# A layer norm on GpSimd that takes the mean from the statistics' tile, without a negated copy from ScalarE

## The chip, the cores and the metric

The kernel runs on one core of one Trainium2 chip. The metric is the device time of one execution in microseconds (us); the time before is 1062.31 us, the median of three runs (1062.3 to 1063.7).

The core has five engines that work side by side, each through its own queue in order: PE (TensorE, matrix products; its weight loads are listed apart as PEld), DVE (VectorE), ACT (ScalarE), POOL (GpSimd) and SP (SyncE, which here only issues DMAs). An instruction that waits for another engine holds up all that stands behind it in its own queue.

## The reference, cut to what matters

Thirty-two batches of a 512 x 128 array `x` go through four graph layers. Each layer first normalizes the rows, then applies its own attention to the result, and adds what comes out to `x`:

```
def _layernorm(x, axis=-1, eps=1e-5):
    m = jnp.mean(x, axis=axis, keepdims=True)
    v = jnp.var(x, axis=axis, keepdims=True)
    return (x - m) / jnp.sqrt(v + eps)
...
h = jnp.maximum(_layernorm(x, axis=-1), 0.0)
x = x + _L0_gnn_ref(h, adj, ...)
h = jnp.maximum(_layernorm(x, axis=-1), 0.0)
x = x + _L1_gnn_ref(h, adj, ...)
... (the same with _L2_gnn_ref and _L3_gnn_ref)
```

The four layers are attention over a 512 x 512 adjacency matrix with different masks and score functions. The norm ahead of them is the same each time, so there are 4 x 32 = 128 of these norms.

## The kernel before, in words

**Tiles.** A batch is held as 128 partitions by 4 chunks (`C`) of 128 values; a partition holds four rows, and a statistic of the batch is a 128 x 4 tile. All batches stay in `xs` from load to output.

**The norm, `preln` (L530).** It has up to five steps:

- `variances` (L503): DVE computes `bn_stats` of each chunk (L511, four instructions) and `bn_aggr` (L513, four instructions). The result `mv` is 128 x 4 x 2: mean and variance side by side.
- `inv_dev` (L518): POOL adds epsilon to the variance (L523, `ve`) and raises it to the power -1/2 (L525, `rstd`).
- `emit_shift`: in the ACT variant (the first eight batches of layer 0) DVE makes -mean x rstd (L541). In the POOL variant (the other 120 norms) ACT makes -mean (L556), a tile of its own named `shift`.
- `norm`: in the ACT variant four activations (L545); in the POOL variant four `tensor_scalar` (L560), each of which adds `shift` and multiplies by `rstd`, both given as one value for each partition.
- PE turns the result `xn` over (four transposes, L421) and ACT applies the Relu on the way out of PSUM (L570, `hT`). `hT` feeds the projection on PE (L595 or L581).

**The order of the work.** The kernel does not issue its work in the order of the code. `Plan.op` collects 5421 operations, each with its engine, an assumed length, what it reads and writes, and a due time (`turn`); one norm in one layer of one batch begins a chain. `Plan.run` (L158) then walks through assumed time: of all engines it takes the operation that can begin first, within 0.05 us the one that is due first, and issues it. Every engine's queue has exactly this order. An operation that waits only for earlier work of low priority is therefore put behind whatever the plan found to be due earlier on that engine. Layer 1 of batch b begins after layer 0 of batch b + 6, layer 2 six batches later, and layer 3 four more (`LAGS`, L70).

**Buffers.** Large tiles come from rooms with a fixed count that the plan keeps account of; `xn` comes from `by_pool` (5 buffers, L320). Small tiles (`mv`, `rstd`, `shift` and others) come from `small` (L308), with 8 buffers for each name. The plan keeps no account of those: when none of the eight is free, the writing instruction waits on the chip. `mv` is taken 192 times (128 norms, and two more statistics in each batch of layer 1), `rstd` 192 times, `shift` 128 times.

Beside the chains there are preparations of the adjacency matrix and of the weights. Where the plan sees PE idle for over 0.6 us it issues transposes of the identity whose result is not used (`idle_products`, L334; 150 of them).

Of the kernel before, what the change touches and what calls it, by code (L numbers as in the profile page):

```python
# [34 lines left out]
ALU = mybir.AluOpType  # L35
# [14 lines left out]
PE, DVE, ACT, POOL, SP = "PE", "DVE", "ACT", "POOL", "SP"  # L50
# [61 lines left out]
class Plan:  # L112
# [17 lines left out]
    def op(self, engine, length, emit, reads=(), writes=(), load=0.0, transfers=0, port=0):  # L130
        slots = list(dict.fromkeys(v.slot for v in (*reads, *writes) if v.slot is not None))
        k = len(self.chains) - 1
        op = Operation(engine, length, emit, k, slots)
        op.load, op.transfers, op.port = load, transfers, port
        for s in slots:
            s.users += 1
        needs = {}
        for v in reads:
            needs.update(dict.fromkeys(v.writers))
        for v in writes:  # L140
            needs.update(dict.fromkeys(v.writers))
            needs.update(dict.fromkeys(v.readers))
        for v in reads:
            v.readers.append(op)
        for v in writes:
            v.writers.append(op)
        for n in needs:
            n.after.append(op)
            if n.chain == k:
                op.way = max(op.way, n.way + n.length + DELAY[n.engine])  # L150
        count, beside, begin, _ = self.chains[k]
        turn = begin + STRETCH * op.way if beside is None else beside[0] + beside[1] * count
        op.turn = (turn, len(self.ops))
        op.missing = len(needs)
        self.chains[-1][0] += 1
        self.ops.append(op)
# [101 lines left out]
def kernel(  # L258
# [28 lines left out]
    nc = tc.nc  # L287
# [13 lines left out]
    def wide(t):  # L301

        return t.rearrange("p c f -> p (c f)")
# [4 lines left out]
    def small(name, shape=(P, C)):  # L308
        return sm.tile(list(shape), F32, name=name, tag=name)
# [19 lines left out]
    op = plan.op  # L329
# [8 lines left out]
    def value(r, name):  # L338
        return Value(Slot(r, name))
# [57 lines left out]
    v_x = [Value() for _ in range(B)]  # L397
# [18 lines left out]
    def turn_op(dst, src, reads, writes):  # L416


        def emit():
            for k in range(C):  # L420
                nc.tensor.transpose(dst(k), src(k), ident)  # L421

        op(PE, 0.44, emit, reads, writes)
# [76 lines left out]
    def dve(length, emit, reads, writes, port=0):  # L500
        op(DVE, length, emit, reads, writes, port=port)

    def variances(src, reads):  # L503

        mv = Value()

        def emit():
            st = small("st", (P, C, 6))
            mv.own = small("mv", (P, C, 2))
            for c in range(C):  # L510
                nc.vector.bn_stats(st[:, c, :], src(c))  # L511
            for c in range(C):
                nc.vector.bn_aggr(mv.own[:, c, :], st[:, c, :])  # L513

        dve(1.1, emit, reads, [mv])
        return mv

    def inv_dev(mv):  # L518
        rstd = Value()

        def emit():
            ve = small("ve")
            nc.gpsimd.tensor_scalar(ve, mv.own[:, :, 1], LN_EPS, 1.0, ALU.add, ALU.mult)  # L523
            rstd.own = small("rstd")
            nc.gpsimd.tensor_tensor(rstd.own, ve, mhalf, ALU.pow)  # L525

        op(POOL, 1.3, emit, [mv], [rstd])
        return rstd

    def preln(b, engine):  # L530

        src = xs[:, b]
        mv = variances(lambda c: src[:, c, :], [v_x[b]])
        rstd = inv_dev(mv)
        shift = Value()
        xn = value(by_act if engine is ACT else by_pool, "xn")
        if engine is ACT:

            def emit_shift():
                shift.own = small("shift")  # L540
                nc.vector.scalar_tensor_tensor(shift.own, mv.own[:, :, 0], -1.0, rstd.own, ALU.mult, ALU.mult)  # L541

            def norm():
                for c in range(C):
                    nc.scalar.activation(  # L545
                        xn.t[:, c, :], src[:, c, :], AF.Identity, bias=shift.own[:, c : c + 1],
                        scale=rstd.own[:, c : c + 1],
                    )

            dve(0.08, emit_shift, [mv, rstd], [shift], port=1)  # L550
            op(ACT, 1.54, norm, [shift, rstd, v_x[b]], [xn])
        else:

            def emit_shift():
                shift.own = small("shift")
                nc.scalar.mul(shift.own, mv.own[:, :, 0], -1.0)  # L556

            def norm():
                for c in range(C):
                    nc.gpsimd.tensor_scalar(  # L560
                        xn.t[:, c, :], src[:, c, :], shift.own[:, c : c + 1], rstd.own[:, c : c + 1],
                        ALU.add, ALU.mult,
                    )

            op(ACT, 0.1, emit_shift, [mv], [shift])
            op(POOL, 1.72, norm, [shift, rstd, v_x[b]], [xn], port=4)
        pt = value(banks, "pt")
        turn_op(lambda k: pt.t[:, k, :], lambda k: xn.t[:, k, :], [xn], [pt])
        hT = value(by_act, "hT")
        op(ACT, 0.49, lambda: nc.scalar.activation(wide(hT.t), wide(pt.t), AF.Relu), [pt], [hT])  # L570
        return hT, pt
# [114 lines left out]

    def layer0(b):
        hT, _ = preln(b, ACT if b < EARLY else POOL)
        if b + AHEAD < B:
            load_x(b + AHEAD)  # L690
# [169 lines left out]

    def layer1(b):
        hT, _ = preln(b, POOL)
        h = project_scored(hT, w1_ext, [v_w1])
        src, v_h = Value(), Value(h[0].slot)
# [77 lines left out]
    def layer2(b):  # L942
        hT, _ = preln(b, POOL)
        h = project_scored(hT, w2_ext, [v_w2])
        po, ssum = attend(h, lambda: h[0].t[:, :, P], h, h, None, None)
        v1 = value(by_dve, "v1")

        rs = Value()

        def emit_rs():  # L950
            rs.own = small("rs")
            nc.vector.reciprocal(rs.own, ssum[0].own)

        dve(0.1, emit_rs, ssum, [rs])
        dve(0.6, lambda: nc.vector.tensor_mul(v1.t, po[0].t, per_chunk(rs.own)), [*po, rs], [v1])  # L955
        op(POOL, 1.25, lambda: nc.gpsimd.tensor_add(v1.t, v1.t, row_of(B_L2)), [v_rows], [v1], port=1)  # L956


        em = value(by_act, "em")
        op(ACT, 0.62, lambda: nc.scalar.activation(em.t, v1.t, AF.Exp, bias=minus1), [v1], [em])  # L960
        op(DVE, 0.6, lambda: nc.vector.scalar_tensor_tensor(em.t, em.t, 1.0, v1.t, ALU.min, ALU.max), [v1], [em], port=1)  # L961
        op(POOL, 1.25, lambda: nc.gpsimd.tensor_add(xs[:, b], xs[:, b], em.t), [em], [v_x[b]], port=1)  # L962
# [399 lines left out]
```

## Time and profile before

| | before |
|---|---|
| median of the runs, us | 1062.31 (1062.3, 1062.31, 1063.7) |
| span of the profiled execution, us | 1062.1 |
| median of the runs less that span, us | 0.2 |
| PE busy, us | 1041.7 |
| PEld busy, us | 966.0 |
| DVE busy, us | 868.5 |
| ACT busy, us | 780.5 |
| POOL busy, us | 776.2 |

The page gives the profiled execution's time as its span, from the first to the last instruction. "Busy" is the time in which an engine has an instruction at work; waits in its queue are not in it. A share of the whole span is an average over a start in which data arrive and the first batches fill the pipeline, a long middle, and an end in which it drains. The stretches are therefore read apart.

In a line of instruction groups stand the source line, the engine, the operation, what it writes and reads, the shape and the count; then busy time in total, the mean duration of one in ns, and the idle time of the engine just before such instructions with what ended it. In a timeline the first number is the start in us, the second the duration of the run of like instructions. A window's line gives the busy time of PE, PEld, DVE, ACT and POOL in that stretch with their instruction counts, then the clock granted to PE, the DMA share and GB/s.

### The profile page before, as it was taken

The page shows a single profiled execution, that of the slowest core. Times are in us where ns is not written, and L with a number is a line of the kernel's source. Part 1 is how long each engine was busy: PE and PEld are TensorE (multiplying, and loading weights), DVE is VectorE, ACT ScalarE, POOL GpSimd, SP SyncE. Part 2 cuts the span into 40 slices and gives each one's busy share as a digit, 9 for nine tenths or more (in the row PEclk, how much of TensorE's full clock was granted, in tenths as well). Part 3 has the DMA queues.
Part 4 walks back from the last instruction along what each step waited for, and adds up shares of the span by engine and source line. Part 5 has one row for each costly group of instructions (what it writes and reads, how often), then busy time and mean ns, then how long its engine had stood idle before and what let it go on. Part 6 is the DMA issues. An engine that isn't in the chain of part 4 may idle for free.

```text
span 1062.1 us, 25166 instructions
## 1 busy us (share of the span) xinstructions
PE 1041.7 (98%) x8475; PEld 966.0 (91%) x8475; DVE 868.5 (82%) x3694; ACT 780.5 (73%) x2024; POOL 776.2 (73%) x1140
## 2 busy tenths in 40 slices
PE   7899999999999999999999999999999999999998
PEld 7789789989999999999999999999899999999997
DVE  7799999989988878888888888888888877766752
ACT  6768897789877777777877777787777777767751
POOL 4489577778787777787778778777877666576772
PEclk9899999999999999999999999999999999999999
DMA  6400000000010000000000000000000000000001
GB/s 181 96 12 2 1 2 21 2 12 11 2 31 2 21 21 21 22 21 12 2 12 11 12 12 12 11 2 11 12 11 11 11 11 11 11 22 11 22 24 37
DMA packets 56912, 20.49 MB, mean 19 GB/s; under 512 B 21584, under 2 KB 56272, under 8 KB 56784
## 3 DMA queue, kind: packets, MB, share of 16 engines
q1 hardware_dynamic: 56784, 18.90, 7.2%
q8 instruction: 67, 1.10, 0.5%
q14 instruction: 61, 0.50, 0.2%
HBM read 10.43 MB, written 8.39 MB: 18 GB/s over the span
## 4 chain that ended last, share of the span: by engine, by line
PE 88%; DVE 4%; POOL 3%; DMA 1%; SPq 1%; issue 1%; ACT 1%; POOLq 0%; DVEq 0%; ACTq 0%
PE po L675 20%; PE pt L421 16%; PE po L984 10%; PE pg L911 10%; PE proj L595 7%; PE po L837 5%; PE prow L421 3%; PE p L581 3%; PE pz L581 3%; PE px L581 3%; PE po L980 3%; PE po L842 2%; PE po L834 1%; PE po L847 1%; POOL xn L560 1%
## 5 line engine op out<-in xcount | busy, mean ns | idle before, releaser
L675 PE MATMUL po<-h,pT 128*128 128x128 f32 x2048 | 242.8, 275 | 0.8 <-DVE pT L664 0.8
L675 PEld LDWEIGHTS po<-h,pT 128*128 128x128 f32 x2048 | 236.4, 192 | 5.8 <-issue 4.1
L560 POOL TENSOR_SCALAR xn<-xs,shift,rstd 128x128 f32<-128x128 f32 x480 | 213.1, 459 | 2.8 <-DVE top L633 0.9
L655 ACT ACTIVATE y<-y,nmax 128x512 f32<-128x512 f32 x256 | 181.7, 714 | 5.3 <-DVE nmax L637 4.6
L525 POOL TENSOR_TENSOR rstd<-ve,mhalf 128x4 f32<-128x4 f32 x160 | 170.9, 1068 | 13.3
L622 DVE CUSTOM_DVE_ANT_0 y<-prow,bias 128x512 f32<-128x512 f32 x256 | 162.8, 683 | 1.6 <-PE prow L421 1.6
L984 PE MATMUL po<-h,offT 128*128 128x128 f32 x1024 | 135.4, 275 | 0.0
L911 PE MATMUL pg<-adjTe,hg 128*128 128x512 f32 x256 | 131.0, 593 | 0.0
L421 PE MATMUL pt<-ident,y 128*128 128x128 f32 x1024 | 130.2, 274 | 0.7 <-ACT hl L819 0.7
L421 PEld LDWEIGHTS pt<-ident,y 128*128 128x128 f32 x1024 | 115.1, 141 | 13.8 <-issue 8.5
L984 PEld LDWEIGHTS po<-h,offT 128*128 128x128 f32 x1024 | 124.6, 192 | 0.0
L511 DVE BATCH_NORM_STATS2 st<-xs 128x6 f32<-128x128 f32 x512 | 109.8, 277 | 7.2 <-POOL xs L962 4.5
L595 PEld LDWEIGHTS proj<-w_ext,hT 128*128 128x128 f32 x768 | 96.8, 192 | 19.0 <-issue 9.6
L595 PE MATMUL proj<-w_ext,hT 128*128 128x130 f32 x768 | 102.9, 277 | 1.4 <-ACT hT L570 1.3
L647 ACT ACTIVATE y<-y,src 128x512 f32<-128x512 f32 x128 | 84.6, 714 | 20.8 <-DVE rmax L622 19.6
L962 POOL TENSOR_TENSOR xs<-xs,em 128x512 f32<-128x512 f32 x32 | 42.0, 1312 | 76.8 <-DVE em L961 63.8
L956 POOL TENSOR_TENSOR v<-v,rows 128x512 f32<-128x512 f32 x32 | 40.9, 1279 | 72.4 <-DVE v L955 72.4
L570 ACT ACTIVATE hT<-pt 128x512 f32<-128x512 f32 x128 | 73.5, 589 | 25.3 <-PE pt L421 14.0
L647 ACT ACTIVATE y<-y,h 128x512 f32<-128x512 f32 x128 | 84.7, 714 | 7.9 <-DVE rmax L622 7.7
L664 DVE TENSOR_TENSOR pT<-pt,adjT 128x512 f32<-128x512 f32 x128 | 82.6, 681 | 5.7 <-PE pt L421 5.6
L421 PE MATMUL pt<-ident,xn 128*128 128x128 f32 x512 | 77.8, 274 | 1.5 <-POOL xn L560 1.3
L412 ACT COPY h<-proj 128x260 f32<-128x260 f32 x192 | 66.1, 371 | 13.4 <-PE proj L595 12.4
(204 smaller groups left out, 2302.3 us busy)
## 6 DMA issues: line engine op xcount, KB each, us to landing
xs<-in_x_dram SPq DMA_DIRECT2D x32, 256.0 KB, 4.0
out_dram<-yo SPq DMA_DIRECT2D x32, 256.0 KB, 2.3
u<-h SPq DMA_DIRECT2D x128, 0.5 KB, 1.8
bias<-in_adj_dram SPq DMA_DIRECT2D x4, 256.0 KB, 4.4
wts<-in_L_gnn_W_dram SPq DMA_DIRECT2D x3, 64.0 KB, 4.2
rows<-in_L_gnn_bias_dram SPq DMA_DIRECT2D x2, 64.0 KB, 3.7
wt_o<-L_gnn_others_weight_dram SPq DMA_DIRECT2D x1, 64.0 KB, 2.5
wts<-n_L_gnn_self_weight_dram SPq DMA_DIRECT2D x1, 64.0 KB, 4.5
```

The costliest lines, as they stand in the source:

```text
L421: nc.tensor.transpose(dst(k), src(k), ident)
L511: nc.vector.bn_stats(st[:, c, :], src(c))
L525: nc.gpsimd.tensor_tensor(rstd.own, ve, mhalf, ALU.pow)
L560: nc.gpsimd.tensor_scalar(xn.t[:, c, :], src[:, c, :], shift.own[:, c : c + 1], rstd.own[:, c : c + 1], ALU.add, ALU.mult,)
L581: nc.tensor.matmul(pt.t[:, c, :], lhsT=column(hT, c), rhs=w, start=True, stop=True)
L595: nc.tensor.matmul(p[:, c, :], lhsT=column(hT, 2 * k + c), rhs=w_ext, start=True, stop=True)
L622: nc.vector.tensor_tensor_reduce(wide(y[ib].t), wide(prow.t), bias[:, ib, :], 1.0, LOWEST, ALU.add, ALU.max, rmax.own[:, ib : ib + 1],)
L647: nc.scalar.activation(yw, yw, AF.Prelu, alpha=0.2, bias=src()[:, ib : ib + 1])
L655: nc.scalar.activation(yw, yw, AF.Exp, bias=nmax.own[:, ib : ib + 1], accum_out=ssum[0].own[:, ib : ib + 1])
L675: nc.tensor.matmul(po[ib].t[:, ib, :], lhsT=pT.t[:, jb, :], rhs=h[0].t[:, jb, 0:P], start=(jb == 0), stop=(jb == C - 1),)
L911: nc.tensor.matmul(wide(pg.t), lhsT=hg.t[:, nb, :], rhs=adjTe[:, nb, :], start=(nb == 0), stop=(nb == C - 1))
L984: nc.tensor.matmul(po[ib].t[:, ib, :], lhsT=offT[:, jb, blk(ib)], rhs=h1.t[:, jb, :], start=False, stop=(jb == C - 1),)
```

## The change

In the POOL variant of `preln` the norm subtracts the mean, read from `mv`, in place of adding `shift`. The ACT operation that made `shift` is left out, and with it the norm's dependence on ACT. The norm now reads `mv` itself, so a buffer of `mv` is in use until the norm is done. The assumed length of the norm stays 1.72. The plan is made anew from the changed list of operations; the ACT variant is as it was.

```diff
@@ preln, the branch for POOL
-            def emit_shift():
-                shift.own = small("shift")
-                nc.scalar.mul(shift.own, mv.own[:, :, 0], -1.0)
-
             def norm():
                 for c in range(C):
                     nc.gpsimd.tensor_scalar(
-                        xn.t[:, c, :], src[:, c, :], shift.own[:, c : c + 1], rstd.own[:, c : c + 1],
-                        ALU.add, ALU.mult,
+                        xn.t[:, c, :], src[:, c, :], mv.own[:, c, 0:1], rstd.own[:, c : c + 1],
+                        ALU.subtract, ALU.mult,
                     )
 
-            op(ACT, 0.1, emit_shift, [mv], [shift])
-            op(POOL, 1.72, norm, [shift, rstd, v_x[b]], [xn], port=4)
+            op(POOL, 1.72, norm, [mv, rstd, v_x[b]], [xn], port=4)
```

## The prediction, made before the changed kernel was run

> **What bounds the kernel now.** I read the windows view first, because the shares of the page average over stages. Two stretches of the middle, then four of the start:
>
> ```profile
> 350.00:400.00 50.00, 50.00 (x415) 46.62 (x414) 42.10 (x159) 38.25 (x98) 34.32 (x53) 1.00 0.05 12
> 750.00:800.00 50.00, 50.00 (x422) 47.27 (x422) 40.97 (x146) 36.72 (x89) 37.83 (x54) 1.00 0.04 11
> ```
>
> ```profile
> 35.00:50.00 15.00, 11.10 (x72) 9.28 (x73) 10.80 (x69) 11.57 (x41) 6.00 (x9) 0.90 0.35 83
> 50.00:75.00 25.00, 23.43 (x180) 21.68 (x179) 22.55 (x116) 13.21 (x46) 21.88 (x37) 0.92 0.09 13
> 75.00:105.00 30.00, 29.80 (x259) 29.21 (x258) 27.81 (x122) 26.21 (x73) 29.31 (x46) 1.00 0.06 10
> 105.00:150.00 45.00, 43.16 (x318) 37.62 (x317) 44.12 (x207) 36.87 (x102) 28.42 (x36) 1.00 0.01 2
> ```
>
> In the middle PE is busy for 50.00 of 50 us, ACT for 38 and POOL for 34 to 38. Less work on ACT buys nothing there. At the start no single engine is full: to 50 us everyone has gaps (POOL works 6.00 of 15 us), from 50 to 105 us POOL is the fullest (51.2 of 55 us), from 105 us DVE (44.1 of 45). So a gain or a loss is made before 150 us or where an engine stops PE.
>
> The chain of waits says the same; POOL carries it in this stretch (norms, powers, the add of L871):
>
> ```profile
> 58.02 1.02 POOL rstd L525
> ...
> 62.23 1.15 POOL h L871
> 63.38 1.74 POOL xn L560 x4
> ...
> 65.81 1.72 POOL xn L560 x4
> ```
>
> **The change, part by part.**
>
> *Removed: 120 ACT instructions (L556).*
>
> ```profile
> L556 ACT ACTIVATE shift<-mv 128x4 f32<-128x4 f32 x120 | 23.0, 205 | 48.3 <-DVE mv L513 25.7 <-DVE rsum L791 9.9 <-POOL xn L560 9.6
> ```
>
> 120 x 205 ns is 24.6 us of durations (23.0 us busy, since neighbours overlap), and ACT stood idle for 48.3 us just before them. All of it lies beside PE, which is full; I cost it at nothing in the middle. Were that cover gone, ACT's 23.0 us would be the most it could give.
>
> *Changed: 480 POOL instructions subtract where they added, and take the mean from `mv`.* No row shows this form. The nearest rows are a subtraction and an addition of two tiles of one size on this engine:
>
> ```profile
> L820 POOL TENSOR_TENSOR hl<-hs,hl 128x256 fp32r<-128x256 f32 x64 | 46.5, 744 | 21.4 <-ACT hl L819 20.6 <-PE proj L595 0.7
> L857 POOL TENSOR_TENSOR xs<-xs,rest 128x256 f32<-128x256 f32 x32 | 24.2, 755 | 36.3 <-DVE nmax L750 16.5 <-ACT rest L852 14.9 <-DVE rs L795 2.1
> ```
>
> Subtraction costs 744 ns, addition 755 ns. So I take no difference from the 448 ns median of L560. The ends are 372 ns (half of the 744 for half the columns; 76 ns less) and 744 ns (the whole row; 296 ns more). What counts is the stretch that POOL fills: the window view of L560 has 36 of them from 50 to 105 us, so the ends are -36 x 76 ns = -2.7 us and +36 x 296 ns = +10.7 us. In the middle POOL works some 36 of 50 us, and even +296 ns for each of about 24 norms in 50 us (7.1 us) would leave it below PE.
>
> *Moved: the first norms of the POOL variant.* This is where I expect the time to change. POOL's timeline:
>
> ```profile
> 35.09 1.23 POOL L525 TENSOR_TENSOR rstd<-ve,mhalf 128x4 f32<-128x4 f32 x1
> ...
> 36.93 1.01 POOL L525 TENSOR_TENSOR rstd<-ve,mhalf 128x4 f32<-128x4 f32 x1
> 42.62 1.44 POOL L820 TENSOR_TENSOR hl<-hs,hl 128x256 fp32r<-128x256 f32 x2 [4.68 <-ACT hl L819]
> ...
> 53.06 1.75 POOL L560 TENSOR_SCALAR xn<-xs,shift,rstd 128x128 f32<-128x128 f32 x4
> ```
>
> and ACT's:
>
> ```profile
> 51.31 0.22 ACT L556 ACTIVATE shift<-mv 128x4 f32<-128x4 f32 x1
> ...
> 56.28 0.59 ACT L556 ACTIVATE shift<-mv 128x4 f32<-128x4 f32 x5
> ```
>
> Eight powers come before 33 us, for the eight ACT norms; those at 35.09 and 36.93 us are the first for norms on POOL (layer 0 of batch 8 and layer 1 of batch 0). Both are complete by 37.94 us, and POOL then stands idle for 4.68 us. Yet ACT makes the first `shift` at 51.31 us and the next five from 56.28 us: the plan put these steps behind ACT's work that was due earlier. Without them both norms are free at 37.94 us. They take 1.75 us (53.06) and 1.72 us (65.81), which the 4.68 us gap holds. So 3.5 us of work leave the packed stretch after 50 us.
>
> What is late next is DVE: it is busy for 25.80 us of the 30 from 50 to 80 us (windows view), so at most 4.2 us can be taken back there before DVE leads. A third norm (power finished at 47.96 us, `shift` among the five at 56.28) might move too, but POOL's next gap is only 1.22 us; 3.5 us is my value, 4.2 the cap. What follows a moved norm moves with it: four transposes, a Relu and a projection on PE and ACT, and for batch 8 four DMAs on SP's queue (4 x 0.6 us), which is idle from 42.22 to 47.91 us.
>
> PE had waits of 1.33 and 0.57 us at 45.5 to 47.8 us, and its granted clock was 0.90 in this stretch. Eight products of L837 take 2.07 us at 48.83 and 1.91 us at 51.12, against 1.06 us at 42.50; with their neighbours (L834, L595) the excess is 2.9 us. If the moved work fills those waits this may go too. I leave it out of the forecast and keep it for the low end.
>
> Two rows bear on where the norms land. The four of 71.55 us took 2.87 us, while DVE ran L1185, L805 and L806, each with two inputs in SBUF. The Trainium skill, SBUF — State Buffer, section Who interferes with whom, speaks against the change here: a DVE instruction with two SBUF inputs blocks a GpSimd instruction that reads SBUF, and DVE runs L805 and L806 at 40.54 us, where the norms would go. By that rule both might take 2.87 us, 5.7 us for a gap of 4.68, and about 1 us of the gain would be lost.
>
> *Added: a longer life for `mv`.* DVE's `bn_aggr` may now wait for a norm on POOL, with all of DVE's queue behind it (scores, `pT`, which PE waits for). I cost it at nothing in the forecast, and price it below.
>
> The sum is -3.5 us against the profiled execution's 1062.1 us, 0.2 us under the median; on the median it is **1058.8 us**.
>
> **The rivals.**
>
> *No change: 1062.3 us.* The early norms only stand waiting. ACT is the engine that delayed `shift`, and ACT also makes the Relu that each of them needs next; DVE is full from 105 us on and may swallow what POOL gives. Against it: ACT is busy only 13.21 of 25 us from 50 to 75 us.
>
> *Slower, by DVE waiting for a buffer of `mv`: 1068.7 us.* Statistics run far ahead: from the end of a `shift` to the start of its norm the median is 42 us. The queue orders pair statistics and norms; so paired, the trace has at most eight `rstd` in use, and eight is all there are. With `mv` held to the norm's end a ninth would be wanted at three places: statistics at 312.5 us against a norm that ends at 313.6, at 807.2 against 809.6, at 832.3 against 835.3. That is 1.0 + 2.4 + 3.0 = 6.4 us of DVE. It decides where the wait is longer than PE's store of ready work. Against it stands a wait of the same kind now:
>
> ```profile
> ACT shift L556 <- POOL xn L560: 9.6, 3, 4.5
> ```
>
> ACT waited 9.6 us for `shift` buffers, 4.5 at the longest, and PE kept on: from 300 to 316 us, around one of them, it was busy 16.00 of 16.
>
> *The subtraction is dear on GpSimd: 1073.0 us,* by the +10.7 us above. The equal pair L820 and L857 speaks against it.
>
> That the change does not do what it says would show as any of the 120 rows of L556 left over, or as a norm that still waits for ACT; I give it no chance of its own.
>
> **How the numbers follow.** About 0.2% (2.1 us) is what a measurement of this kernel can tell from no change. The forecast case has 0.46, of which 0.42 is faster by more than that and 0.04 within. No change has 0.22, of which 0.20 within and 0.02 slower. The wait for `mv` has 0.24, the dear subtraction 0.08; both are slower. Besides, the plan is made anew, and any stretch of the start may fall differently; that is why the first case has no more. Faster 0.42, within 0.24, slower 0.34. The low end is -4.2 (DVE's cap) - 2.9 (clock) = 1055.2; POOL's -2.7 us would lie under the same cap. The high end takes in the dear subtraction's bound, 1073. The likeliest case alone reaches from 1055 to 1060.
>
> **What would show it.** Right: no L556; first POOL norms at 38 to 42 us; POOL less packed from 50 to 75 us; L560 still at 448 ns; PE at 50.00 in the middle. Wrong: POOL idle at 38 to 42 us as before (then another step holds the norms), DVE's L513 waiting for POOL's L560 with PE below 50.00 at the same time, or L560 well above 448 ns.

## The result and the profile after

| | before | after |
|---|---|---|
| median of the runs, us | 1062.3 (4 runs, 1061.67 to 1063.7) | 1189.42 (4 runs, 1187.99 to 1193.06) |
| span of the profiled execution, us | 1062.1 | 1186.3 (its time: 1187.99) |

The changed kernel is slower: 1.1201 times the time of before (95% interval 1.1182 to 1.122), 127.1 us. The forecast was 1058.8 us in a range that ended at 1073.

The page of the changed kernel, busy time by engine:

```profile
PE 1084.8 (91%) x8447; PEld 985.0 (83%) x8447; DVE 882.5 (74%) x3694; ACT 764.5 (64%) x1904; POOL 946.9 (80%) x1140
```

POOL has the same 1140 instructions as before and works 170.7 us longer on them (946.9 less 776.2). ACT has the 120 instructions fewer that the diff says. The costliest group of POOL is the norm, first before, then after:

```profile
L560 POOL TENSOR_SCALAR xn<-xs,shift,rstd 128x128 f32<-128x128 f32 x480 | 213.1, 459 | 2.8 <-DVE top L633 0.9 <-DVE res L937 0.9 <-PE pt L421 0.7
```

```profile
L556 POOL TENSOR_SCALAR xn<-xs,mv,rstd 128x128 f32<-128x128 f32 x480 | 391.2, 826 | 0.5
```

(L556 was the `shift` line before; in the changed kernel this number is the norm's, L560 of before.) One norm instruction takes 826 ns on average and 792 ns at the median; before it was 459 and 448. By busy time the row grew by 178.1 us (391.2 less the 213.1 of before), which covers all of POOL's increase. (Its busy time is less than 480 x 826 ns, as neighbours overlap.)

The windows, first the two stretches of the middle, then the one of the start that the forecast was to relieve:

```profile
350.00:400.00 50.00, 48.41 (x384) 43.36 (x383) 42.38 (x162) 38.23 (x93) 44.81 (x54) 1.00 0.05 12
750.00:800.00 50.00, 45.62 (x352) 41.22 (x351) 38.34 (x147) 31.63 (x79) 41.54 (x50) 0.97 0.03 6
```

```profile
50.00:75.00 25.00, 19.80 (x150) 18.13 (x151) 16.73 (x89) 11.47 (x38) 23.86 (x31) 0.93 0.07 13
```

PE had 50.00 of 50 us in both stretches of the middle, and now has 48.41 and 45.62. The important column is the one in brackets behind it: PE gets 384 and 352 instructions done where it did 415 and 422. POOL works 45 and 42 of 50 us: more than before, and still not all of the time. From 50 to 75 us POOL is more packed and not less: 23.86 of 25 us, where it was 21.88. So an engine that is not full holds PE up. The waits view names the way:

```profile
ACT zn L922 <- POOL rstd L525: 68.3, 23, 5.0
PEld pt L421 <- POOL xn L556: 54.9, 100, 1.9
...
PE po L979 <- ACT h L412: 35.5, 12, 3.0
...
DVE mv L513 <- POOL xn L556: 12.5, 4, 4.4
```

(The columns are the us waited, how often, and the longest.) PE waits for norms directly, at its weight loads 100 times; and 12 times it waits 3 us for `h`, which ACT makes late because ACT was waiting for a power from POOL. DVE's wait for `mv`, the rival that the prediction priced at 6.4 us, is there too, but is a small part.

The first norms of the POOL variant, from POOL's timeline:

```profile
34.30 1.23 POOL L525 TENSOR_TENSOR rstd<-ve,mhalf 128x4 f32<-128x4 f32 x1
35.64 3.13 POOL L556 TENSOR_SCALAR xn<-xs,mv,rstd 128x128 f32<-128x128 f32 x4
...
40.27 3.49 POOL L556 TENSOR_SCALAR xn<-xs,mv,rstd 128x128 f32<-128x128 f32 x4
```

They begin at 35.64 and 40.27 us, where the two norms that the prediction wanted early had begun at 53.06 and 65.81; so the move that the forecast was built on did happen. But a norm (four instructions) now lasts 3.13 or 3.49 us, where it had lasted 1.75.

### The profile page after: what moved, and what is told of

Read it like the earlier page. It is cut to its first block, busy times and chain, and to the rows that moved or that the text cites. A ratio compares the mean times of both kernels' runs of the same rounds, so it can differ in the third digit from the quotient of the medians.

```text
span 1186.3 us, 25075 instructions
## 1 busy us (share of the span) xinstructions
PE 1084.8 (91%) x8447; PEld 985.0 (83%) x8447; DVE 882.5 (74%) x3694; ACT 764.5 (64%) x1904; POOL 946.9 (80%) x1140
## 5 line engine op out<-in xcount | busy, mean ns | idle before, releaser
L556 POOL TENSOR_SCALAR xn<-xs,mv,rstd 128x128 f32<-128x128 f32 x480 | 391.2, 826 | 0.5
L979 PE MATMUL po<-h,offT 128*128 128x128 f32 x1024 | 151.3, 296 | 35.5 <-ACT h L412 35.5
L525 POOL TENSOR_TENSOR rstd<-ve,mhalf 128x4 f32<-128x4 f32 x160 | 166.4, 1040 | 13.4
L979 PEld LDWEIGHTS po<-h,offT 128*128 128x128 f32 x1024 | 139.0, 211 | 37.9 <-ACT h L412 37.8
L421 PE MATMUL pt<-ident,xn 128*128 128x128 f32 x512 | 98.6, 286 | 36.6 <-POOL xn L556 33.9
L421 PEld LDWEIGHTS pt<-ident,xn 128*128 128x128 f32 x512 | 64.0, 142 | 61.3 <-POOL xn L556 54.9
L412 ACT COPY pT<-pt 128x512 f32<-128x512 f32 x64 | 35.8, 587 | 89.5 <-PE pt L421 89.5
```

The lines of the kernel that those rows point to most:

```text
L556: nc.gpsimd.tensor_scalar(xn.t[:, c, :], src[:, c, :], mv.own[:, c, 0:1], rstd.own[:, c : c + 1], ALU.subtract, ALU.mult,)
L979: nc.tensor.matmul(po[ib].t[:, ib, :], lhsT=offT[:, jb, blk(ib)], rhs=h1.t[:, jb, :], start=False, stop=(jb == C - 1),)
```

## The experiments

The diff changes three things together: the operation (subtraction for addition), the place of the operand (`mv`, a 128 x 4 x 2 tile, with the longer life of its buffers), and the order of every queue, since the plan is made anew. Theory 1: the subtraction itself is dear on this engine, wherever its scalar lies. Theory 2: the scalar's place in `mv` makes the instruction slow. Theory 3: the norm is not dearer, and the loss comes from the other order and the longer life of `mv`. Beside them stands the question how 170.7 us on an engine that is 80% busy become 127 us of the whole. Each time is set against runs of the kernel before on the same chip, with medians of 1061.87, 1062.7 and 1062.89 us in the three groups.

**1. sub_from_copy: the operation alone.** The kernel before, with its order, its queues and its `shift` tile; ACT's copy no longer negates, and POOL subtracts it.

```diff
-                nc.scalar.mul(shift.own, mv.own[:, :, 0], -1.0)
+                nc.scalar.mul(shift.own, mv.own[:, :, 0], 1.0)
...
-                        ALU.add, ALU.mult,
+                        ALU.subtract, ALU.mult,
```

> The kernel before, with two edits that cancel: ScalarE's step copies the mean without the sign, and the norm subtracts it. Order, plan and buffers are those of before; only the operation differs. Theory 1 (GpSimd's subtraction with a per-partition value is dear): the norm at about 790 ns, as in the changed kernel's 792, and a time well above 1100 us. Theory 2 (reading the mean from the statistics' tile, where it stands beside the variance, is dear): the norm at 448 ns and 1062 us. Theory 3 (the longer life of the statistics' buffers and the other order): 448 ns and 1062 us as well.

Measured: 1177.47 us, 1.1085 times before [1.1067, 1.1102], +115.6 us. The group of the norm in this kernel:

```profile
L560 POOL TENSOR_SCALAR xn<-xs,shift,rstd 128x128 f32<-128x128 f32 x480 | 390.6, 826 | 0.2
```

826 ns again, without `mv` and in the old order. Theories 2 and 3 fall as the main cause: the operation by itself costs 115.6 us in the old order. As the queues are those of before and only a duration differs, this kernel is also where to see how the time is lost. POOL's timeline of before, then of sub_from_copy, at the same place in the order:

```profile
513.48 5.17 POOL L560 TENSOR_SCALAR xn<-xs,shift,rstd 128x128 f32<-128x128 f32 x12
518.62 1.27 POOL L919 TENSOR_TENSOR hgb<-hg,rows 128x512 f32<-128x512 f32 x1
520.26 1.36 POOL L525 TENSOR_TENSOR rstd<-ve,mhalf 128x4 f32<-128x4 f32 x1
```

```profile
521.94 9.86 POOL L560 TENSOR_SCALAR xn<-xs,shift,rstd 128x128 f32<-128x128 f32 x12
531.77 1.28 POOL L919 TENSOR_TENSOR hgb<-hg,rows 128x512 f32<-128x512 f32 x1
533.74 1.03 POOL L525 TENSOR_TENSOR rstd<-ve,mhalf 128x4 f32<-128x4 f32 x1
```

The plan puts three norms in a row. They took 5.17 us and now take 9.86, and the power behind them ends 4.7 us later for it. What stands behind that power, from ACT's timeline, first of before:

```profile
521.66 1.28 ACT L927 ACTIVATE zn<-zn,rstd 128x128 f32<-128x128 f32 x4 [0.30 <-POOL rstd L525]
...
524.68 0.56 ACT L412 COPY h<-p 128x512 f32<-128x512 f32 x1
```

```profile
534.80 1.28 ACT L927 ACTIVATE zn<-zn,rstd 128x128 f32<-128x128 f32 x4 [4.97 <-POOL rstd L525]
...
537.82 0.56 ACT L412 COPY h<-p 128x512 f32<-128x512 f32 x1
```

ACT waits 4.97 us for the power in place of 0.30. The copy `h` begins 3.02 us after `zn` in both kernels, so it is late by as much. PE's timeline goes on from there, first of before:

```profile
525.63 1.06 PE L984 MATMUL po<-h,offT 128*128 128x128 f32 x8
```

```profile
538.44 1.53 PE L984 MATMUL po<-h,offT 128*128 128x128 f32 x8 [2.95 <-ACT h L412]
539.76 0.64 PE L980 MATMUL po<-wts,own 128*128 128x128 f32 x2
540.19 1.91 PE L984 MATMUL po<-h,offT 128*128 128x128 f32 x8
...
543.52 1.06 PE L984 MATMUL po<-h,offT 128*128 128x128 f32 x8
```

PE stands for 2.95 us. Its next two sets of eight products take 1.53 and 1.91 us and the third 1.13; then it is 1.06 us again, as each time at this place before. The clock column of the windows goes with it:

```profile
538.00:541.00 3.00, 2.56 (x14) 2.56 (x15) 2.04 (x10) 3.00 (x11) 2.07 (x4) 0.68 0.05 6
541.00:545.00 4.00, 4.00 (x28) 3.76 (x27) 1.13 (x8) 2.14 (x8) 4.00 (x6) 0.81 0.06 0
545.00:550.00 5.00, 5.00 (x45) 4.76 (x44) 3.78 (x18) 0.84 (x3) 3.57 (x5) 1.00 0.16 52
```

The granted clock is 0.68 and 0.81 after the wait and then 1.00. (In finer windows it is 0.50 from 540 to 542 us and 1.00 from 543 to 545.) The wait is paid for twice.

**2. add_from_mv: the order and the place, without the operation.** The changed kernel with the addition put back; it leaves out the sign of the mean.

```diff
-                        ALU.subtract, ALU.mult,
+                        ALU.add, ALU.mult,
```

> The changed kernel with the norm adding the mean where it should subtract it; this leaves the sign of the mean out of the computation. Plan, order and buffers are those of the changed kernel. Theory 1: the norm back at 448 ns; the time then is that of the rest of the change, 1058.8 us by my forecast (first norms earlier), up to 1068.7 us if VectorE's waits for the statistics' buffers reach TensorE. Theory 2: 792 ns and about 1189 us. Theory 3: 448 ns, but a time that stays near 1189 us.

Measured: 1076.24 us, 1.013 times before [1.0105, 1.0156], +14.4 us. The norm takes 463 ns, so reading `mv` costs POOL nothing. This is the kernel that the prediction believed it was forecasting, a norm at the old price in the new order, and it is slower too. The first norms, from POOL's timeline:

```profile
36.35 1.75 POOL L556 TENSOR_SCALAR xn<-xs,mv,rstd 128x128 f32<-128x128 f32 x4
...
39.57 2.17 POOL L556 TENSOR_SCALAR xn<-xs,mv,rstd 128x128 f32<-128x128 f32 x4
```

They fill the gap as forecast, in 3.9 us. What did not follow is the gain. Two windows of before, then the same of add_from_mv:

```profile
80.00:90.00 10.00, 10.00 (x88) 9.77 (x87) 9.56 (x42) 9.71 (x27) 9.83 (x18) 1.00 0.01 2
140.00:150.00 10.00, 10.00 (x92) 10.00 (x91) 9.97 (x50) 8.39 (x26) 6.36 (x11) 1.00 0.01 3
```

```profile
80.00:90.00 10.00, 6.64 (x45) 5.73 (x46) 7.19 (x30) 10.00 (x27) 9.85 (x13) 0.96 0.01 2
140.00:150.00 10.00, 5.19 (x36) 3.89 (x34) 8.12 (x37) 9.75 (x28) 5.43 (x7) 1.00 0.01 2
```

From 80 to 90 us POOL does 13 instructions in the place of 18 in the same busy time: longer ones come first. Over 0 to 150 us PE is busy for 125.62 us where it was 135.87, and from 350 to 950 us for 598.16 of 600. Of the ten us less at the start 2.6 are idle products, whose number the plan sets (110 for 131, 14.03 us for 16.65); 7.6 us are real work. So most of the loss is at the start, in an order of which the early norms are only one part.

**3. sub_true_length: the plan is told.** The changed kernel with the assumed length of the norm at its measured four times 792 ns, 3.17 us; what is computed is the same.

```diff
-            op(POOL, 1.72, norm, [mv, rstd, v_x[b]], [xn], port=4)
+            op(POOL, 3.17, norm, [mv, rstd, v_x[b]], [xn], port=4)
```

> The changed kernel, with the norm's assumed length in the plan at its measured 3.17 us (four times 792 ns) in place of 1.72. If the loss comes from queues laid out for a norm of 1.72 us, so that TensorE stands behind norms that are late, the time falls to 1080 to 1130 us. If GpSimd simply has too much to do (947 us busy), it stays within 15 us of 1189 us.

Measured: 1104.67 us, 1.0399 times before [1.0383, 1.0416]; of the 127.1 us, 42.8 are left. Its page and the middle in one window:

```profile
PE 1065.3 (97%) x8571; PEld 978.8 (89%) x8571; DVE 886.2 (80%) x3694; ACT 771.1 (70%) x1904; POOL 948.6 (86%) x1140
```

```profile
350.00:950.00 600.00, 595.16 (x4833) 547.79 (x4832) 498.13 (x2033) 436.20 (x1053) 559.12 (x664) 1.00 0.05 13
```

POOL has the same 948.6 us of work, and from 350 to 950 us it is even busier than in the changed kernel (559.12 against 496.19 of 600 us); yet PE is at 595.16 in place of 548.50. So it is not POOL's work as such that stops PE in the middle, but its place in the queues.

**4. forms: the price by itself.** The kernel before, with 88 POOL instructions added whose results nobody uses: eight of each form on tiles of 128 partitions.

```diff
+    for _ in range(8):
+        ts(to[:, 0:128], src[:, 0:128], s, m, ALU.add, ALU.mult)
+    for _ in range(8):
+        ts(to[:, 0:128], src[:, 0:128], s, m, ALU.subtract, ALU.mult)
...
+    for _ in range(8):
+        ts(to[:, 0:32], src[:, 0:32], s, m, ALU.subtract, ALU.mult)
```

> The kernel before with 88 GpSimd instructions behind its end, eight of each form, on 128 columns (the last two forms on 32): add then multiply, subtract then multiply, the same two with the first value from a tile of pairs, multiply then add, multiply then subtract, multiply twice, add or subtract then multiply with constants. Theory 1: every form with a subtraction at about 790 ns and the others at 448; the tile of pairs makes no difference. Theory 2: the two forms that read the tile of pairs at 790 ns, subtraction from the plain tile at 448. On 32 columns theory 1 expects a subtraction some 85 ns above an addition if the price goes by the column, 340 ns if by the instruction.

The added instructions stood in POOL's queue at 755 to 822 us, not at the end as meant; the span of this single run is 1109.1 us, which says nothing of the change. The answer is in the durations (least, median, most, in ns), one source line for each form:

```profile
L1338 POOL TENSOR_SCALAR biasT<-xs,one x8: 447/448/472, 755.2 to 759.1; 128x128 f32<-128x128 f32 x8
```

```profile
L1340 POOL TENSOR_SCALAR biasT<-xs,one x8: 792/792/802, 759.6 to 766.4; 128x128 f32<-128x128 f32 x8
```

```profile
L1344 POOL TENSOR_SCALAR biasT<-xs,two,one x8: 792/794/795, 771.7 to 782.4; 128x128 f32<-128x128 f32 x8
```

```profile
L1348 POOL TENSOR_SCALAR biasT<-xs,one x8: 789/792/1425, 789.1 to 798.3; 128x128 f32<-128x128 f32 x8
```

```profile
L1354 POOL TENSOR_SCALAR biasT<-xs x8: 642/642/652, 806.6 to 811.7; 128x128 f32<-128x128 f32 x8
```

```profile
L1356 POOL TENSOR_SCALAR biasT<-xs,one x8: 366/366/367, 812.4 to 816.8; 128x32 f32<-128x32 f32 x8
```

```profile
L1358 POOL TENSOR_SCALAR biasT<-xs,one x8: 472/472/477, 817.3 to 822.5; 128x32 f32<-128x32 f32 x8
```

L1338 adds and then multiplies: 448 ns. L1340 subtracts and then multiplies: 792 ns. L1344 is L1340 with the scalar in a tile of pairs, as `mv` is: 794 ns; theory 2 falls a second time. L1348 multiplies and then subtracts: 792 ns, so the order of the two doesn't matter. L1354 subtracts with constants in the instruction: 642 ns (addition with constants, L1352: 297). L1356 and L1358 are addition and subtraction on 32 columns: 366 and 472 ns. So the price goes by the column: addition (448 - 366) / 96 = 0.85 ns, subtraction (792 - 472) / 96 = 3.33 ns. On 32 columns the difference is 106 ns where 85 was expected, so a small part of it does not go by the column.

The Trainium skill, GPSIMD Engine Reference, section 3.1 (Elementwise — side-by-side cycle accounting), gives 1.03 cycles per element for a body with k ≤ 2; I take k as the number of operations, which is two here. At the 1.2 GHz that it counts with, addition's 0.85 ns is 1.02 cycles and agrees; subtraction's 3.33 ns is 4.0 cycles and does not. Here the measurement decides.

**5. sub_one_of_four and sub_two_of_four: how the price becomes time.** The kernel before with the subtraction in one or in two of the four chunks of each norm (there the sign of the mean is left out).

```diff
-                        ALU.add, ALU.mult,
+                        ALU.subtract if c < 1 else ALU.add, ALU.mult,
```

> The kernel before, with the first of a norm's four instructions subtracting in place of adding (its value has the wrong sign there, so the sign of the mean is left out in one chunk of four). Order and plan as before; GpSimd has 120 x 345 ns = 41 us more to do. If GpSimd's spare time in the middle hides it, as my prediction had it, only the packed start shows it: 1062 to 1066 us. If every microsecond by which a burst of norms is late reaches TensorE's queue, a quarter of sub_from_copy's 116 us: about 1091 us.

> As sub_one_of_four, with two of the four instructions subtracting: 83 us more on GpSimd. If the loss is in proportion, about 1120 us; if there is a store of ready work that covers the first part, one of four costs under 10 us and two of four well under half of the 116, below 1110 us.

Measured: 1079.85 us, 1.0164 [1.0148, 1.0179], between the two times expected, and 1102.67 us, 1.0379 [1.0362, 1.0395]. The middle, in order: before, one of four, two, and all four (sub_from_copy):

```profile
350.00:950.00 600.00, 600.00 (x4923) 557.70 (x4922) 493.37 (x2033) 446.73 (x1134) 450.47 (x659) 1.00 0.05 12
```

```profile
350.00:950.00 600.00, 592.98 (x4837) 548.51 (x4835) 498.04 (x2015) 440.53 (x1120) 472.28 (x655) 1.00 0.05 12
```

```profile
350.00:950.00 600.00, 578.73 (x4709) 534.07 (x4708) 480.00 (x1976) 425.29 (x1091) 493.97 (x646) 1.00 0.05 12
```

```profile
350.00:950.00 600.00, 551.99 (x4315) 505.57 (x4316) 449.36 (x1841) 392.17 (x1017) 496.73 (x593) 0.97 0.05 11
```

Already the first quarter costs PE 7.0 us here, though POOL works only 472 of 600 us with one chunk changed. Two rows of PE's group list, the products L984 and the norm's transposes, of before and of sub_from_copy:

```profile
L984 PE MATMUL po<-h,offT 128*128 128x128 f32 x1024 | 135.4, 275 | 0.0
L421 PE MATMUL pt<-ident,xn 128*128 128x128 f32 x512 | 77.8, 274 | 1.5 <-POOL xn L560 1.3
```

```profile
L984 PE MATMUL po<-h,offT 128*128 128x128 f32 x1024 | 150.3, 295 | 35.4 <-ACT h L412 35.4
L421 PE MATMUL pt<-ident,xn 128*128 128x128 f32 x512 | 97.2, 284 | 33.6 <-POOL xn L560 33.1
```

From such rows (all in us, over the whole span, as the difference from before; L980 are the products that stand between those of L984):

| chunks that subtract | POOL busy | PE idle before L984 | L984 and L980 themselves | PE idle before and busy in the norm's transposes | sum of the three | span |
|---|---|---|---|---|---|---|
| 1 | +45.1 | +6.9 | +1.3 | +4.8 | 13.0 | +17.3 |
| 2 | +90.4 | +20.5 | +1.3 | +13.2 | 35.0 | +40.7 |
| 4 (sub_from_copy) | +171.0 | +35.4 | +18.3 | +51.5 | 105.2 | +114.9 |

The three columns of PE account for most of the span's growth in each row. With thirteen waits of up to 1.7 us (two chunks) L984 itself hardly changes; with twelve of up to 3.0 us (four chunks) its products take 295 ns in the place of 275, which goes with the lowered clock of experiment 1. And the transposes wait for the norm chunk by chunk and come one at a time. So the second half of the dose costs more than the first.

**6. add_mv_old_order, add_from_mv_16: the longer life of `mv`.** The first is the kernel before in which ACT's operation issues nothing and POOL adds the mean from `mv`: the plan and its order are those of before, and the buffers of `mv` are held as in the change. The second is add_from_mv with 16 buffers of `mv`. Both leave out the sign of the mean.

```diff
-            op(ACT, 0.1, emit_shift, [mv], [shift])
+            op(ACT, 0.1, lambda: None, [mv], [shift])
...
-                        xn.t[:, c, :], src[:, c, :], shift.own[:, c : c + 1], rstd.own[:, c : c + 1],
+                        xn.t[:, c, :], src[:, c, :], mv.own[:, c, 0:1], rstd.own[:, c : c + 1],
```

> As add_from_mv (the norm adds the mean from the statistics' tile; the sign of the mean is left out), but the plan keeps an empty operation where ScalarE's step stood, so every engine's queue is in the order of the kernel before, without the 120 ScalarE instructions. If the 14 us of add_from_mv (1076.2 against 1061.9) come from the new order, this is at 1060 to 1063 us; the empty place also keeps the first norms late. If they come from VectorE waiting for statistics' buffers that the norm now holds, it stays at 1068 to 1076 us.

> As add_from_mv, with 16 buffers for the statistics' tile in place of 8, so that VectorE never waits for a norm (6.3 us, three waits, in add_from_mv). Order and plan as in add_from_mv. If the order costs the 14 us: 1072 to 1077 us. If the buffers do: back to 1062 us or, with the early norms that I forecast, 1059.

Measured: 1065.46 us, 1.0028 [1.0017, 1.0039], between the two ranges expected, and 1072.23 us, 1.0097 [1.0073, 1.0121]. What DVE's `bn_aggr` waits for in add_from_mv, from the view of its line:

```profile
  POOL xn L556: 6.3, 3
```

6.3 us in three waits, and the same in add_mv_old_order; the prediction had worked out 6.4 us in three. In add_mv_old_order PE stays full around two of them (20.00 us of 300 to 320, 17.00 of 825 to 842) and loses 0.5 us around the third (14.48 of 800 to 815, where it was 15.00). That kernel is 2.8 us slower than before. The size holds two things, the waits and ACT's missing 120 steps, which were not taken apart; without those steps it is at any rate not faster. In the new order 16 buffers bring about 4 us (1076.24 less 1072.23; the intervals of the two overlap, so this size is loose).

**7. shift_len_02, neg_on_dve: other orders.** The first is the kernel before with one assumed length doubled, and nothing else. In the second, DVE makes the negated mean, in 120 instructions of its own.

```diff
-            op(ACT, 0.1, emit_shift, [mv], [shift])
+            op(ACT, 0.2, emit_shift, [mv], [shift])
```

```diff
-                nc.scalar.mul(shift.own, mv.own[:, :, 0], -1.0)
+                nc.vector.tensor_scalar(shift.own, mv.own[:, :, 0], -1.0, None, ALU.mult)
...
-            op(ACT, 0.1, emit_shift, [mv], [shift])
+            dve(0.08, emit_shift, [mv], [shift], port=1)
```

> The kernel before, with the assumed length of ScalarE's step at 0.2 us in place of 0.1 (its measured length is 0.205). No instruction is added or removed; only the plan's order changes. It shows what a new order by itself can do to this kernel: if orders are harmless, 1062 us within 2; if the 14 us of add_from_mv are of the kind that any new order may bring, a move of 3 to 15 us, either way.

> The kernel before, with the negated mean made by VectorE (120 instructions of some 150 ns) and not by ScalarE. The norm still adds, statistics' buffers are let go early, and the first norms no longer wait for ScalarE's queue. If early first norms help, as I forecast, 1058 to 1061 us, less what 18 us more of VectorE take back; if early norms are what costs add_from_mv its 14 us, 1070 to 1078 us.

Measured: 1069.99 us, 1.0074 [1.0059, 1.0089], and 1065.65 us, 1.0032 [1.0021, 1.0043]; the second lies between the two ranges expected. shift_len_02 issues the very instructions of before, and loses 7.3 us by their order alone. The window from 50 to 100 us, of before and of shift_len_02:

```profile
50.00:100.00 50.00, 48.43 (x395) 46.29 (x394) 45.36 (x225) 37.74 (x115) 46.19 (x76) 0.96 0.07 12
```

```profile
50.00:100.00 50.00, 43.19 (x315) 40.22 (x315) 39.12 (x184) 31.60 (x91) 46.39 (x74) 0.90 0.07 12
```

PE does 80 instructions fewer in it. neg_on_dve was meant to bring the norms early without `mv`'s longer life, but its first norm on POOL is at 47.7 us, hardly early, so it does not decide whether early norms help.

**8. add_long_plan: what the true length costs as an order.** add_from_mv (without the sign of the mean) with the assumed length of sub_true_length: its order, with the norms at their old price.

```diff
-            op(POOL, 1.72, norm, [mv, rstd, v_x[b]], [xn], port=4)
+            op(POOL, 3.17, norm, [mv, rstd, v_x[b]], [xn], port=4)
```

> sub_true_length with the fast addition: the plan takes 3.17 us for a norm, the chip 1.74 (the sign of the mean is left out). The order is that of sub_true_length. If the 43 us by which sub_true_length is above the kernel before are GpSimd's real load, this falls to 1062 to 1080 us; if they are the price of the order that such a plan makes, it stays at 1095 to 1105 us.

Measured: 1083.56 us, 1.0194 [1.0177, 1.0211], +20.7 us, between the two ranges expected. sub_true_length, with the same order and the dear norms, is at 1104.67: 21.1 us more. So of its 42.8 us about half is the order that the plan makes for long norms, and half is the norms' own load. The order's half lies at the start again: without idle products PE works 108.1 us of the first 150 (130.88 less 22.77), where before it works 119.2 (135.87 less 16.65), and from 350 to 950 us it has 599.25 of 600.

No kernel of this study is faster than the kernel before.

## Why the prediction was wrong

The sum of the causes: the operation 115.6 us (experiment 1), the new order with the longer life of `mv` 14.4 us (experiment 2); together 130.0, where 127.1 was measured, and the two need not add exactly. By the prediction's steps:

- **Removed: nothing speaks against it.** Without ACT's 120 steps, in the old order, the kernel is not faster (experiment 6, where the waits for `mv` come in too).
- **Changed, the price: wrong.** "Subtraction costs 744 ns, addition 755 ns. So I take no difference from the 448 ns median of L560." The two rows are of `tensor_tensor`, and the norm is a `tensor_scalar`: 792 ns, +344 at the median, outside even the upper end of +296. The pair that looked like evidence said that subtracting is no dearer in another instruction, one whose 256 columns take 2.9 ns each whichever of the two it does. No row of before had a `tensor_scalar` that subtracts on POOL; the upper end was the only honest bound, and it was given 0.08.
- **Changed, the cover: wrong, and this is the step that failed most.** "In the middle POOL works some 36 of 50 us, and even +296 ns for each of about 24 norms in 50 us (7.1 us) would leave it below PE." By this the dear subtraction was worth 10.7 us, and with the true +344 ns it would have been 36 x 344 = 12.4 us. It was 115.6 (experiment 1). In the middle POOL does stay below PE (in sub_from_copy 496.73 us against 551.99, of 600), but the share of a stretch says nothing of the place in a queue: the norms stand three in a row ahead of a power that ACT waits for, ACT's wait delays the copy behind it, and PE waits for that copy. Of the 114.9 us by which sub_from_copy's span grew, PE lost 53.7 that way (35.4 and 18.3) and 51.5 at the norms' own transposes, which wait for the late norms directly. An order made for 1.72 us stayed as it was; a quarter of the price already cost 17.0 us (experiment 5). The "24 norms in 50 us" are 24 instructions, six norms, so the 7.1 us were added up rightly; it is the comparison with PE's time that did not bear on the matter.
- **Moved: the mechanism was right, the gain was not there.** The norms begin at 36.35 and 39.57 us in add_from_mv and fill POOL's gap. That kernel should then have been at 1058.8 us; it is at 1076.24. The forecast cut two norms out of the packed stretch and left all else in place, but the plan put everything behind them anew, and the new start is worse by 7.6 us of PE's real work. How much of that the early norms did themselves was not separated; the runs show that each of the other orders tried here lost too (shift_len_02, add_long_plan, and neg_on_dve with its longer work on DVE). The prediction also called POOL the fullest engine from 50 to 105 us, with 51.2 of 55 us; by the same rows PE has 53.2 (23.43 and 29.80), of which 5.1 are idle products, all before 75 us. From 75 to 105 us PE was the fullest, so POOL had less to give there than the forecast took.
- **The shared reads of DVE and POOL.** The second group of early norms, beside DVE's instructions with two inputs in SBUF, took 2.17 us (L800 of DVE ran from 39.77 us for 0.79); the first took 1.75, as before. This one pair agrees in sign with the rule that the prediction cited (the Trainium skill, SBUF — State Buffer, Who interferes with whom); the 2.87 us feared for both was too much.
- **Added: the waits were right to a tenth of a us, and their price too high.** In add_mv_old_order, which has the order that the prediction worked with, DVE waits 0.97, 2.36 and 3.00 us for `mv`, where 1.0, 2.4 and 3.0 were forecast. That kernel is 2.8 us slower and not 6.4; in the new order the waits are worth about 4.
- **The clock at the start:** 1.00 from 0 to 50 us in add_from_mv; 0.97 before. Kernels in the order of before, whose first POOL norm comes at 53 us, show 0.93 (sub_one_of_four), 0.97 (sub_from_copy) and 1.00 (add_mv_old_order) there. So a difference of this size shows no gain of the change.

Open remains whether the two early norms alone, with every other instruction in its old place, would have gained the 3.5 us. That was not tried.

## What to carry to other kernels

Take the price of an operation from a row of the same instruction; a like operation in another instruction is a guess, and on POOL adding a negated value was far cheaper than subtracting. A share of busy time below 100% does not cover a longer instruction where the queues have a fixed order: look at what stands behind it in its queue, who waits for that, and how early that is finished now; and if the instruction does grow, tell the planner (84.3 us of 127.1 came back that way). Where a planner makes the order anew, a gain of a few us can hardly be forecast by moving two operations on paper: one assumed length, with nothing else changed, moved this kernel by 7.3 us.

## What the runs showed of the hardware that was not expected

- POOL's `tensor_scalar` with a subtraction takes 3.33 ns a column, with an addition 0.85; on 128 columns 792 against 448 ns (forms). Two values given for each partition cost 150 ns more than two constants (448 against 297, 792 against 642).
- After PE had stood for 2.95 us (sub_from_copy) its granted clock was 0.68 over 3 us and 0.81 over the 4 us after, and eight products took up to 1.91 us in the place of 1.06. Where the waits were 1.7 us at the longest (sub_two_of_four) the products of that line took 276 ns on average, against 275.
